# A two-layer relational graph convolution: 70 of 3126 tiles of source rows fetched by SyncE and ScalarE, a transfer per row

## The chip, the cores and the metric

The kernel runs on one core of a Trainium2 chip. The metric is the device time of one execution in microseconds; the time of a kernel is the median over several executions. A core has a matrix engine (TensorE, written PE, with its weight loads as PEld), a vector engine (VectorE, DVE), a scalar engine (ScalarE, ACT), a general one (GpSimd, POOL) and one for synchronisation (SyncE, SP). Each works through its own list of instructions in order. SP, ACT and POOL also issue the transfers (DMAs) between HBM and the on-chip memory SBUF; PE writes its results to PSUM.

## What is computed

There are N = 12500 nodes with C = 128 features, and E = 200000 edges sorted by their destination. Each edge has one of 10 types, the position of the largest of ten of its attributes. A layer takes, for each node and each type, the mean of the source nodes' features over the edges that arrive with that type, multiplies each mean by the type's 128x128 weights and sums over the types; to this come the node's own features times `root`, and a bias. Two such layers, with a relu between them, are followed by a sum with the input and a layer norm. Everything is in fp32.

```python
def _rgcn_layer(x, src, dst, edge_type, w_rel, root, bias):
    N = x.shape[0]
    seg = dst * NUM_REL + edge_type
    xs = x[src]
    sums = jax.ops.segment_sum(xs, seg, num_segments=N * NUM_REL)
    cnt = jax.ops.segment_sum(jnp.ones(seg.shape, x.dtype), seg, num_segments=N * NUM_REL)
    mean = (sums / jnp.maximum(cnt, 1.0)[:, None]).reshape(N, NUM_REL, -1)
    return jnp.einsum('nrd,rdo->no', mean, w_rel) + x @ root + bias
edge_type = jnp.argmax(msg[:, NODE_EMB_DIM:-NODE_EMB_DIM], axis=1).astype(jnp.int32)
h = jax.nn.relu(_rgcn_layer(x, src, dst, edge_type, w_rel1, root1, b1))
y = _rgcn_layer(h, src, dst, edge_type, w_rel2, root2, b2)
out = _layernorm(x + y)
```

## The kernel before

The edges are cut into 1563 tiles of 128, and the tiles into groups: 97 of 16 tiles, one of 8 and one of 3, so 99 a layer. A tile of the sorted edges reaches few nodes, and the kernel works in windows of 12 nodes by 10 types, 120 columns a tile. For a group it does this:

- `gather`: POOL issues one indirect transfer per tile (line 445), which brings the 128 source rows of 512 bytes from the table (`x` in the first layer, the stored hidden features `hD` in the second) into a tile of the buffer `g`. There are RING = 3 such buffers of 16 tiles.
- `sums`: DVE builds for each tile a matrix `oh` (line 461) that has the edge's weight, one over its count, in the column of its node and type; two `at` matrices (line 465) say where the windows lie. PE multiplies rows by `oh` into PSUM, `zp` (line 468), one matmul per tile. A fp32 matmul shows as two passes in the profile. The matmuls of a group are issued from j = 15 down to j = 0; 15 and the following ones are held in program order, and the waits for all gathers of the group are put on the first issued. ACT copies the sums out of PSUM in 4 pieces, `zs` (line 482).
- `project`, one group later: PE multiplies the sums by the weights of the 10 types, 20 matmuls into `pp` (line 494); ACT copies these out as `ms` (line 500).
- `add`, one group later again: two matmuls of `at` by `ms` (line 510) lay the windows out over 160 nodes, and DVE adds them to the running result `acc` (line 516) at an address that it loads into a register.

`layer` runs this over the groups. A gather into `g` must wait until the zp matmuls of three groups before have read that buffer; zp has one buffer in PSUM, `oh` and `zs` have two, `at` and `ms` three. When the edges of a block of 512 nodes are through, which is the case about every fourth group, the block is finished: SP loads its input rows (`rows_dma`, line 371), PE transposes them (line 386), ACT copies the transposed block out (`fT`, line 388), PE multiplies by `root` (line 400) and adds `acc` (line 401), ACT applies the relu (`hb`, line 414; first layer) or the square root of the norm (`rstd`, line 432; second), and SP stores the block. The first layer also has work on the edges' types and counts, spread over the groups in 13 chunks of 128 tiles: SP loads destinations, attributes and keys (lines 125, 290, 302, 330), ACT copies keys (line 335), DVE compares (line 341) and PE counts (lines 343 and 345).

The order on each engine is not the order of the text: a scheduler places the instructions, and only those marked with `keep_in_program_order` keep their places. A transfer issued by SP or ACT signals its end on one of 8 completion semaphores ("lanes") that the two engines use in turn, and an issue on a lane waits until the transfer before it on that lane has ended.

Of the kernel before, what the change touches and what calls it, by code (L numbers as in the profile page):

```python
# [9 lines left out]
F32 = mybir.dt.float32  # L10
BF16 = mybir.dt.bfloat16
I32 = mybir.dt.int32
# [4 lines left out]
DRAM = bass.MemoryType.DRAM  # L17
DVE = mybir.EngineType.DVE
SP = mybir.EngineType.SP

P = 128
NREL = 10
# [3 lines left out]
KW = NREL * WN  # L26
G = 16
QB = 4
HT = 8
HR = HT * WN  # L30
SW = 160
RING = 3
DB = 8
L = 40
CT = 128
# [8 lines left out]
def rgcn_resnorm_kernel(ctx: ExitStack, tc: tile.TileContext, x, src, dst, attr, w_rel1, root1, b1,  # L44
# [14 lines left out]
    nc = tc.nc  # L59
    N, C = x.shape  # L60
    E = src.shape[0]
    D = attr.shape[1]
    CE = CT * P
    NT = -(-E // P)
# [3 lines left out]
    t = NT // G * G  # L68
# [31 lines left out]
    fast = ctx.enter_context(ExitStack())  # L100
    keep = fast.enter_context(tc.tile_pool(name="keep", bufs=1))
    prep = fast.enter_context(tc.tile_pool(name="prep", bufs=1))
    eqp = fast.enter_context(tc.tile_pool(name="eqp", bufs=2))
    gpool = fast.enter_context(tc.tile_pool(name="gpool", bufs=RING))
    dpool = fast.enter_context(tc.tile_pool(name="dpool", bufs=2))
    zpool = fast.enter_context(tc.tile_pool(name="zpool", bufs=2))
    spool = fast.enter_context(tc.tile_pool(name="spool", bufs=3))
# [5 lines left out]
    idxE = keep.tile([P, NCH * CT], I32, name="idxE")  # L113
# [29 lines left out]
    def then(engine, ins):  # L143

        if engine in loaded:
            loaded.remove(engine)
            tc.keep_in_program_order(ins)
        return ins
# [81 lines left out]
    for k, (t, n) in list(enumerate(groups))[full:]:  # L230
        if k > full:
            nc.scalar.dma_start(bt[:, k:k + 1], bass.AP(dst.tensor, dst.offset + t * P, [[1, 1], [1, 1]]))
        m = n if t + n < NT else n - 1
# [91 lines left out]
    def count(c):  # L325
# [11 lines left out]
        R = P + L  # L337
        for d in range(1, L + 1, DB):
            eq = eqp.tile([P, DB, R], BF16, name="eqb")
            ahead = bass.AP(kh.tensor, kh.offset + d, [[kh.ap[0][0], p], [1, DB], [1, R]])  # L340
            nc.vector.tensor_tensor(eq[:p], kp[:p, None, :R].to_broadcast([p, DB, R]), ahead, op=ALU.is_equal)  # L341
            for k in range(0, DB, 4):
                nc.tensor.matmul(pc[:p], identb[:p, :p], eq[:p, k:k + 4, L:], start=(d + k == 1), stop=False)  # L343
# [18 lines left out]
    def rows_dma(sb, dr, k, store):  # L362
# [7 lines left out]
        for a, b in pairs:  # L370
            then("SP", nc.sync.dma_start(b, a) if store else nc.sync.dma_start(a, b))

# [67 lines left out]

    HELD = "clamped to a node on the chip"

    def gather(table, t0, n):
        g = gpool.tile([P, G, C], F32, name="g")
        return g, [then("POOL", nc.gpsimd.indirect_dma_start(  # L445
            out=g[:, j, :], out_offset=None, in_=table, in_offset=bass.IndirectOffsetOnAxis(
                ap=idxE[:, t0 + j:t0 + j + 1], axis=0))) for j in range(n)]

    whole = mybir.DependencyInfo(mybir.DependencyClass.Sync, mybir.DependencyReason.DATA)

    def halves(n):
        return [(h, min(HT, n - h * HT)) for h in range(-(-n // HT))]

    def sums(table, k, end):

        t0, n = groups[k]
        g, gathers = gather(table, t0, n)
        oh = dpool.tile([P, G, KW], F32, name="oh")
        for j in range(n):
            t = t0 + j  # L460
            then("DVE", nc.vector.tensor_scalar(oh[:, j, :], iotaP[:, :KW], keyE[:, t:t + 1], wE[:, t:t + 1],  # L461
                                                op0=ALU.is_equal, op1=ALU.mult))
        at = spool.tile([HR, 2, SW], F32, name="at")
        for h, _ in halves(n):
            nc.vector.tensor_scalar(at[:, h, :], iotaP[:HR], place[:, h, k:k + 1], None, op0=ALU.is_equal)  # L465
        zp = ps_z.tile([P, G // QB, YB], F32, name="zp")
        for j in range(n) if end else reversed(range(n)):
            m = nc.tensor.matmul(zp[:, j // QB, j % QB * KW:(j % QB + 1) * KW], g[:, j, :], oh[:, j, :],  # L468
                                 start=True, stop=True)
            then("PE", m)  # L470
            if end:
                continue
            if j < n - 1:
                tc.keep_in_program_order(m)
                continue

            for d in gathers[:j]:
                tc.add_manual_dep(m.ins, d.ins.name, whole, reason="one wait per group")
        zs = zpool.tile([P, NREL, G, WN], F32, name="zs")
        for b in range(-(-n // QB)):  # L480
            m = min(QB, n - b * QB)
            then("ACT", nc.scalar.activation(  # L482
                zs[:, :, b * QB:b * QB + m, :],
                zp[:, b, :m * KW].rearrange("c (j r n) -> c r j n", r=NREL, n=WN), AF.Copy))
        return k, zs, at

    def project(l, k, zs, at):

        n = groups[k][1]
        po = ps_o.tile([P, 2, C], F32, name="pp")  # L490
        ms = spool.tile([HR, 2, C], F32, name="ms")
        for h, m in halves(n):
            for r in range(NREL):
                nc.tensor.matmul(po[:m * WN, h], zs[:, r, h * HT:h * HT + m].rearrange("c j n -> c (j n)"),  # L494
                                 wsb[l][:, r, :], start=(r == 0), stop=(r == NREL - 1))
        if n % HT:
            for h, m in halves(n):
                nc.scalar.activation(ms[:m * WN, h], po[:m * WN, h], AF.Copy)
        else:
            nc.scalar.activation(ms[:, :n // HT], po[:HR, :n // HT], AF.Copy)  # L500
        return k, ms, at
# [3 lines left out]
    def add(k, ms, at):  # L505

        pa = ps_o.tile([P, 2, C], F32, name="pp").rearrange("p h c -> p (h c)")[:, :SW]
        parts = halves(groups[k][1])
        for h, m in parts:
            nc.tensor.matmul(pa, ms[:m * WN, h], at[:m * WN, h], start=(h == 0), stop=(h == len(parts) - 1))  # L510
        if not offs:
            offs.extend(nc.values_load_multi_w_load_instructions(
                bt[0:1, k:min(NG, k + 4)], engines=[DVE], min_val=0, max_val=N - 1,
                skip_runtime_bounds_check_because=HELD)[1])
        s = ds(offs.pop(0), SW)
        nc.vector.tensor_tensor(acc[:, s], acc[:, s], pa, op=ALU.add)  # L516

    def layer(table, l, finish, steps, flag_too=False):

        done = 0  # L520
        held, projected = [], []
        ready = flag = None

        def project_oldest():
            projected.append(project(l, *held.pop(0)))

        def add_oldest():
            nonlocal done
            k, ms, at = projected.pop(0)
            add(k, ms, at)  # L530
            while done < NBLK and sum(groups[k]) >= done_after(done):
                finish(done, ready if done == NBLK - 1 else block_in(done, l))
                done += 1

        for k in range(NG):
            end = k >= NG - 2
            if projected:
                add_oldest()
            if end:

                if held:
                    project_oldest()
                if not ready:
                    ready = block_in(NBLK - 1, l)
                    if flag_too:
                        loads, (flag,) = nc.values_load_multi_w_load_instructions(
                            flag_i[0:1, 0:1], min_val=0, max_val=1, skip_runtime_bounds_check_because=HELD)
                        for ld in loads:
                            tc.keep_in_program_order(ld)
                        loaded.update(("POOL", "DVE", "PE", "ACT", "SP"))  # L550
            held.append(sums(table, k, end))
            if end and projected:
                add_oldest()
            if len(held) > 1:
                project_oldest()
            if steps:
                till, left, s = steps[0]
                for _ in range(max(1, -(-left[0] // max(1, till - k)))):
                    left[0] -= 1
                    if next(s, steps) is steps:  # L560
                        steps.pop(0)
                        break
        while held or projected:
            if held:
                project_oldest()
            if projected:
                add_oldest()
        return flag
# [5 lines left out]
    def as_steps(f, c):  # L574
        f(c)
        yield
# [5 lines left out]
    for a in range(0, NPAD, YB):  # L582
        m = min(NPAD - a, YB)
# [7 lines left out]
    for c in range(1, NCH):  # L591
        s = [as_steps(sources, c + 1), types(c + 1)] if c + 1 < NCH else []
        todo.append((c * CT // G - 1, [8 + L // DB + 2], chain(*s, count(c))))
    layer(x, 0, hidden, todo)
    def flagged():

# [32 lines left out]
    def each_tile(before, stages):  # L629

        with tc.For_i(0, E, GT) as e:
# [30 lines left out]
            nw = nc.values_load(bw[0:1, 1:2], min_val=1, max_val=-(-N // W), skip_runtime_bounds_check_because=HELD)  # L662
            b0 = nc.values_load(bw[0:1, 0:1], engines=[DVE, SP], min_val=0, max_val=N - 1,
                                skip_runtime_bounds_check_because=HELD)
# [108 lines left out]
```

## Time and profile before

| what | value |
|---|---|
| median of 3 runs | 4760.23 us (4756.89 to 4762.15) |
| profiled execution | 4772.34 us, span 4770.4 us |
| mean granted TensorE clock | 0.739 |
| gathers | 3126, of 0.944 us each |
| traffic of POOL's queue (q0) | 100032 packets, 205.07 MB |
| HBM read, written | 262.28 MB, 13.60 MB |

The profile is taken by the hardware from one execution. A group line has the engine and the kernel's line, what is written and read, the count, the busy time and the mean of one instruction, and after a second bar the idle time ahead of those instructions with what ended most of it: "issue" where the engine waited for nothing that the profile shows, "remote" where the releasing event is on another engine but not identified, or the name of the instruction that released it. In the timeline a line is a run of like instructions: start, length, engine, line, and in brackets the idle time before it. An engine name with a q (SPq, ACTq) stands for the issue of transfers. The chain of waits, followed back from the end, puts 34% of the span down to releases that it can't name, 33% to PE, 21% to issue and 11% to DVE.

### The profile page before, as it was taken

The numbers are of one execution on the slowest core, as the hardware profiler recorded it, in microseconds if no ns is written. First come the engines' busy times: TensorE is split into PE (matmuls) and PEld (weight loads), VectorE is DVE, ScalarE is ACT, GpSimd is POOL, SyncE is SP. The second block draws the span as 40 slices with busy tenths as digits, with TensorE's granted clock in tenths as the row PEclk, the third lists the DMA queues.
The fourth block names the chain that finished last, engine by engine and source line by source line (L and its number), as shares of the span: only waits on it lengthen the run. The fifth ranks groups of instructions, "written<-read, shape, count | busy, mean of one in ns | idle before, by whom it ended". The sixth has DMA issues, their size and how long they took to land.

```text
span 4770.4 us, 43637 instructions
## 1 busy us (share of the span) xinstructions
PE 2759.5 (58%) x16162; PEld 2520.6 (53%) x16162; DVE 1511.5 (32%) x4652; ACT 527.0 (11%) x1136; POOL 2955.2 (62%) x3142
## 2 busy tenths in 40 slices
PE   2455556555655555666645555666655656565656
PEld 1455555555554545555544555555555555555556
DVE  5233333333333333333222222222222223222323
ACT  1011111111111101111110111111111111111111
POOL 5666665666656666666546666666666666666663
PEclk9677777777777777777776777777777777777778
DMA  4122122122221221212111211221222222222211
GB/s 141 44 79 74 50 74 74 50 75 62 61 77 47 75 62 51 57 48 52 46 49 46 54 52 51 53 56 51 52 56 53 52 52 58 51 52 52 58 52 40
DMA packets 180554, 279.00 MB, mean 58 GB/s; under 512 B 55623, under 2 KB 127190, under 8 KB 177206
## 3 DMA queue, kind: packets, MB, share of 16 engines
q0 software_dynamic: 100032, 205.07, 16.9%
q1 hardware_dynamic: 75428, 69.58, 4.6%
q8 instruction: 132, 2.16, 0.2%
q10 hardware_dynamic: 4872, 1.45, 0.1%
q14 instruction: 90, 0.74, 0.1%
HBM read 262.28 MB, written 13.60 MB: 58 GB/s over the span
## 4 chain that ended last, share of the span: by engine, by line
another core or an unknown queue 34%; PE 33%; issue 21%; DVE 11%; ACT 1%; DMA 0%; DVEq 0%; ACTq 0%; SPq 0%
PE pp L494 16%; PE zp L468 11%; DVE oh L461 7%; PE pp L510 2%; PE pf L401 1%; PE pf L400 1%; DVE at L465 1%; ACT zs L482 1%; DVE acc L516 1%; PE pf L343 0%; PE pf L345 0%; PE pf L386 0%; DVE o L436 0%; DVE st L429 0%
## 5 line engine op out<-in xcount | busy, mean ns | idle before, releaser
L445 POOL DMA_INDIRECT g<-in_x_dram,idxE x1563 | 1475.9, 944 | 911.2 <-issue 445.8
L445 POOL DMA_INDIRECT g<-hD,idxE x1563 | 1476.6, 945 | 865.3 <-issue 455.6
L494 PE MATMUL pp<-w,zs 128*96 128x128 f32 x7840 | 1358.2, 336 | 860.4 <-issue 722.1
L494 PEld LDWEIGHTS pp<-w,zs 128*96 128x96 f32 x7840 | 1232.0, 212 | 982.9 <-issue 834.6
L461 DVE TENSOR_SCALAR oh<-bank,keyE,wE 128x120 f32<-128x120 f32 x3126 | 1000.1, 400 | 644.6 <-remote 576.6
L468 PE MATMUL zp<-oh,g 128*128 128x120 f32 x6252 | 1033.5, 325 | 293.5 <-issue 259.9
L468 PEld LDWEIGHTS zp<-oh,g 128*128 128x128 f32 x6252 | 983.1, 240 | 314.0 <-issue 292.5
L482 ACT ACTIVATE zs<-zp 128x480 f32<-128x480 f32 (+1 forms) x782 | 382.9, 575 | 2167.7 <-remote 1912.9
L516 DVE TENSOR_TENSOR acc<-acc,pp 128x160 f32 x198 | 63.7, 322 | 1634.4 <-remote 1043.0
L510 PE MATMUL pp<-at,ms 96*128 96x160 f32 (+1 forms) x784 | 198.1, 386 | 591.1 <-issue 405.0
L510 PEld LDWEIGHTS pp<-at,ms 96*128 96x128 f32 (+1 forms) x784 | 142.5, 232 | 633.8 <-issue 437.1
L500 ACT ACTIVATE ms<-pp 96x256 f32<-96x256 f32 x196 | 74.1, 378 | 1241.3 <-remote 861.3
L341 DVE TENSOR_TENSOR eqb<-pf,kh 128x1344 bf16<-128x1344 f32 (+1 forms) x65 | 100.6, 1552 | 181.4 <-PE pf L345 82.3
L400 PE MATMUL pf<-root,fT 128*128 128x128 f32 x388 | 110.1, 379 | 79.0 <-issue 49.1
L401 PE MATMUL pf<-ident,a 128*128 128x128 f32 x392 | 114.0, 388 | 60.3 <-DVE a L395 22.0
L400 PEld LDWEIGHTS pf<-root,fT 128*128 128x128 f32 x388 | 87.0, 276 | 91.2 <-issue 55.8
L465 DVE TENSOR_SCALAR at<-bank,place 96x160 f32<-96x160 f32 x392 | 131.9, 376 | 0.0
L401 PEld LDWEIGHTS pf<-ident,a 128*128 128x128 f32 x392 | 90.7, 285 | 68.6 <-issue 24.6
L426 DVE TENSOR_TENSOR v<-pf,xb 128x512 f32<-128x512 f32 (+1 forms) x28 | 17.4, 620 | 243.2 <-remote 238.3
L348 DVE TENSOR_REDUCE wp<-pf 128x128 f32<-128x512 f32 (+1 forms) x13 | 9.0, 691 | 182.9 <-remote 175.5
L343 PE MATMUL pf<-eqb,identb 128*128 128x512 bf16 (+1 forms) x130 | 50.5, 388 | 17.9 <-DVE f L320 17.0
L388 ACT ACTIVATE fT<-pf 128x512 f32<-128x512 f32 (+1 forms) x56 | 30.2, 539 | 207.1 <-remote 151.3
(107 smaller groups left out, 483.0 us busy)
## 6 DMA issues: line engine op xcount, KB each, us to landing
m<-in_edge_attr_dram SPq DMA_DIRECT2D x24, 1344.0 KB
g<-in_x_dram,idxE POOLq DMA_INDIRECT x1563
g<-hD,idxE POOLq DMA_INDIRECT x1563
xb<-in_x_dram SPq DMA_DIRECT2D x46, 256.0 KB
hD<-hb SPq DMA_DIRECT2D x23, 256.0 KB
hb<-hD SPq DMA_DIRECT2D x23, 256.0 KB
out_dram<-o SPq DMA_DIRECT2D x23, 256.0 KB
w<-in_L_gnn_w_rel_dram ACTq DMA_DIRECT2D x2, 640.0 KB
```

The source lines that it names most:

```text
L341: nc.vector.tensor_tensor(eq[:p], kp[:p, None, :R].to_broadcast([p, DB, R]), ahead, op=ALU.is_equal)
L400: nc.tensor.matmul(pr[:h, t, :], fT[:, t * P:t * P + h], rsb[l], start=True, stop=False)
L401: nc.tensor.matmul(pr[:h, t, :], a[:, t * P:t * P + h], ident, start=False, stop=True)
L445: return g, [then("POOL", nc.gpsimd.indirect_dma_start(out=g[:, j, :], out_offset=None, in_=table, in_offset=bass.IndirectOffsetOnAxis(ap= ...
L461: then("DVE", nc.vector.tensor_scalar(oh[:, j, :], iotaP[:, :KW], keyE[:, t:t + 1], wE[:, t:t + 1], op0=ALU.is_equal, op1=ALU.mult))
L465: nc.vector.tensor_scalar(at[:, h, :], iotaP[:HR], place[:, h, k:k + 1], None, op0=ALU.is_equal)
L468: m = nc.tensor.matmul(zp[:, j // QB, j % QB * KW:(j % QB + 1) * KW], g[:, j, :], oh[:, j, :], start=True, stop=True)
L482: then("ACT", nc.scalar.activation(zs[:, :, b * QB:b * QB + m, :], zp[:, b, :m * KW].rearrange("c (j r n) -> c r j n", r=NREL, n=WN), AF.C ...
L494: nc.tensor.matmul(po[:m * WN, h], zs[:, r, h * HT:h * HT + m].rearrange("c j n -> c (j n)"), wsb[l][:, r, :], start=(r == 0), stop=(r == ...
L500: nc.scalar.activation(ms[:, :n // HT], po[:HR, :n // HT], AF.Copy)
L510: nc.tensor.matmul(pa, ms[:m * WN, h], at[:m * WN, h], start=(h == 0), stop=(h == len(parts) - 1))
L516: nc.vector.tensor_tensor(acc[:, s], acc[:, s], pa, op=ALU.add)
```

## The change

Some tiles are no longer gathered by POOL. In each layer SP takes tile 64, 128, ... 1536 (24 tiles, always the tile j = 0 of every fourth group) and ACT takes tile 160, 288, ... 1440 (11 tiles, j = 0 of every eighth group, in groups that have no SP tile). For such a tile the engine loads its 128 source numbers into one SBUF row, reads them eight at a time into registers, and issues 128 transfers of one row of 512 bytes each, at the table's row that the register names, into a `rows` tile of which there are two per engine. The issue is spread over the groups ahead of the one that needs the tile: 32 rows per group on SP and 16 per group on ACT, in the order of the program's text. In all 70 of 3126 gathers go, and 6144 row transfers on SP and 2816 on ACT come, with 70 loads of sources and 1120 loads of registers. The zp matmul of j = 0 in these groups reads `rows` in place of `g`.

```diff
+ACT = mybir.EngineType.Activation
...
 RING = 3
+MS = 64
+MA = 128
+RB = 8
...
+    rpool = fast.enter_context(tc.tile_pool(name="rpool", bufs=2))
...
+    by_rows = {}
+
+    def fetch(table, engine, eng, tag, tiles, M):
+
+        lists = {}
+
+        def sources_of(t):
+            lo = min(t * P, E - P)
+            lists[t] = rpool.tile([1, P], I32, name="sr" + tag)
+            then(tag, eng.dma_start(lists[t], src[lo:lo + P].rearrange("(o e) -> o e", o=1)))
+
+        step = 0
+        sources_of(tiles[0])
+        for t in tiles:
+            while step < (t - M) // G:
+                step += 1
+                yield
+            sr = lists.pop(t)
+            if t + M in tiles:
+                sources_of(t + M)
+            r = by_rows[t] = rpool.tile([P, C], F32, name="rows" + tag)
+            for e in range(0, P, RB):
+                loads, at = nc.values_load_multi_w_load_instructions(
+                    sr[0:1, e:e + RB], engines=[engine], min_val=0, max_val=N - 1,
+                    skip_runtime_bounds_check_because="sources are nodes")
+                for ld in loads:
+                    tc.keep_in_program_order(ld)
+                for i in range(RB):
+                    eng.dma_start(r[e + i:e + i + 1, :], table[ds(at[i], 1), :])
+                if (e + RB) % (P * G // M) == 0:
+                    step += 1
+                    yield
+
     def gather(table, t0, n):
         g = gpool.tile([P, G, C], F32, name="g")
-        return g, [then("POOL", nc.gpsimd.indirect_dma_start(
+        return g, {j: then("POOL", nc.gpsimd.indirect_dma_start(
             out=g[:, j, :], out_offset=None, in_=table, in_offset=bass.IndirectOffsetOnAxis(
-                ap=idxE[:, t0 + j:t0 + j + 1], axis=0))) for j in range(n)]
+                ap=idxE[:, t0 + j:t0 + j + 1], axis=0))) for j in range(n) if t0 + j not in by_rows}
 
     whole = mybir.DependencyInfo(mybir.DependencyClass.Sync, mybir.DependencyReason.DATA)
 
...
             nc.vector.tensor_scalar(at[:, h, :], iotaP[:HR], place[:, h, k:k + 1], None, op0=ALU.is_equal)
         zp = ps_z.tile([P, G // QB, YB], F32, name="zp")
         for j in range(n) if end else reversed(range(n)):
-            m = nc.tensor.matmul(zp[:, j // QB, j % QB * KW:(j % QB + 1) * KW], g[:, j, :], oh[:, j, :],
+            rows = by_rows.pop(t0 + j) if t0 + j in by_rows else g[:, j, :]
+            m = nc.tensor.matmul(zp[:, j // QB, j % QB * KW:(j % QB + 1) * KW], rows, oh[:, j, :],
                                  start=True, stop=True)
             then("PE", m)
             if end:
...
                 tc.keep_in_program_order(m)
                 continue
 
-            for d in gathers[:j]:
+            for d in [d for i, d in gathers.items() if i < j]:
                 tc.add_manual_dep(m.ins, d.ins.name, whole, reason="one wait per group")
         zs = zpool.tile([P, NREL, G, WN], F32, name="zs")
         for b in range(-(-n // QB)):
...
                 finish(done, ready if done == NBLK - 1 else block_in(done, l))
                 done += 1
 
+        fetches = [fetch(table, SP, nc.sync, "SP", range(MS, NT - G, MS), MS),
+                   fetch(table, ACT, nc.scalar, "ACT", range(MA + MS // 2, NT - G, MA), MA)]
         for k in range(NG):
+            for f in fetches:
+                next(f, None)
             end = k >= NG - 2
             if projected:
                 add_oldest()
```

## The prediction

> **What bounds the kernel now.** I read the busy table first (median of the runs shown 4760.23 us; the profiled execution is 4772.34 us with a span of 4770.4, and every sum below is made against this span).
>
> ```profile
> PE 2759.5 (58%) x16162; PEld 2520.6 (53%) x16162; DVE 1511.5 (32%) x4652; ACT 527.0 (11%) x1136; POOL 2955.2 (62%) x3142
> L445 POOL DMA_INDIRECT g<-in_x_dram,idxE x1563 | 1475.9, 944 | 911.2 <-issue 445.8
> L445 POOL DMA_INDIRECT g<-hD,idxE x1563 | 1476.6, 945 | 865.3 <-issue 455.6
> L482 ACT ACTIVATE zs<-zp 128x480 f32<-128x480 f32 (+1 forms) x782 | 382.9, 575 | 2167.7 <-remote 1912.9
> ```
>
> No engine is full; POOL is the busiest. Its gathers are 0.944 us each, with about 0.3 us of issue before the next, so 1.249 us apart; half of its idle time is that issue, the other half pauses. ACT's copies of the sums out of PSUM (zs) idle for "remote", mostly. Second, the timeline of two groups of 16 gathers (start, length, engine, line; in brackets the idle time before):
>
> ```profile
> 2508.67 0.94 POOL L445 DMA_INDIRECT g<-hD,idxE  x1 [0.30 <-issue]
> 2512.82 1.96 ACT L482 ACTIVATE zs<-zp 128x480 f32<-128x480 f32 x4 [21.14 <-remote]
> 2512.82 2.58 DVE L461 TENSOR_SCALAR oh<-bank,keyE,wE 128x120 f32<-128x120 f32 x8 [17.47 <-remote]
> 2513.05 0.94 POOL L445 DMA_INDIRECT g<-hD,idxE  x1 [3.44 <-remote]
> ...
> 2519.17 4.92 PE L468 MATMUL zp<-oh,g 128*128 128x120 f32 x32
> ...
> 2523.93 1.69 PE L494 MATMUL pp<-w,zs 128*96 128x128 f32 x14
> ...
> 2530.08 0.80 PE L494 MATMUL pp<-w,zs 128*96 128x128 f32 x3 [2.25 <-issue]
> ...
> 2535.87 1.96 ACT L482 ACTIVATE zs<-zp 128x480 f32<-128x480 f32 x4 [20.84 <-remote]
> 2536.05 0.94 POOL L445 DMA_INDIRECT g<-hD,idxE  x1 [3.31 <-remote]
> ```
>
> The reader is to see one **release** per group: zs on ACT, oh on DVE and the next gather on POOL start together, at 2512.82 and again 23.05 us later. Between them POOL makes 16 x 1.249 = 20.0 us of gathers and then waits 3.3 us. The zp matmuls that ought to release them were over at 2519.17 + 4.92 = 2524.1, yet the release came 11.8 us later, 3.3 us after POOL had gone quiet. PE has two paces: for some 12 us behind a release its passes follow at 0.12 to 0.2 us (14 in 1.69), and from then until POOL stops they come singly with gaps near 0.7, 1.4 and 2.1 us: 10 passes in the 9.9 us from 2525.85 to 2535.74. So the cycle is POOL's 20.0 us plus 3.3. Third, the waits of POOL over the second layer:
>
> ```profile
> POOL g L445 <- issue: 455.6, 1464, 5.1
> POOL g L445 <- remote: 229.0, 64, 8.1
> POOL g L445 <- PE zp L468: 147.8, 30, 8.3
> ```
>
> Pauses cost 229.0 + 147.8 = 377 us of a layer (some 94 of them, 4.0 us each): groups in which a block of nodes is also finished (every fourth) pause 5 to 6 us and last about 25; the two zs copies at 2792.45 and 2817.84 stand 25.4 apart around one. In the first layer the counting chunks bring pauses of 8 to 10.7.
>
> **The change, part by part.**
>
> *Removed:* 35 gathers a layer, 70 in all. One is worth 1.249 us where POOL sets the cycle: at most 87 us. Where the pause rather than POOL ends last, it may be worth nothing; of the 48 tiles that go to SP 36 lie in groups with a long pause, of the 22 that go to ACT one does. (I laid each tile's group against POOL's pause behind the same group in the trace.) Lower end, the other 33 alone: 41.
>
> *Added:* per tile one list of sources (one DMA), 16 register loads of 8 addresses each, and 128 one-row transfers, each with a register instruction before it. No such transfer is in the trace. One-partition DMAs are issued in 0.22 us (SP L221) to 0.47, pairs of larger ones on SP follow at 0.38 to 0.48 while POOL gathers; a register instruction on DVE takes 0.07, a load of a few registers there 0.34, or 0.04 per row. So a row is 0.33 to 0.55 us; I take **0.45**, and 0.70, PE's slow step, as the far bound. Each row also waits for one of 8 completion lanes that both queues share: a load of 128 rows of 512 bytes lands 2.0 us after its issue here, so 8 lanes pass a row per 0.25 us, or 0.5 for each queue while both send, which is hardly dearer than taken. The rows for these two:
>
> ```profile
> 1.66 0.22 SPq L221 DMA_DIRECT2D KD<-negs  x1
> 0.83 0.40 SPq L125 DMA_DIRECT2D s_i<-in_src_dram  x1
> ```
>
> ```profile
> 2.82 0.28 DVE L162 CAST s_f<-s_i 128x128 f32<-128x128 int32 x1 [1.18 <-DMA s_i<-in_src_dram]
> ```
>
> A tile is 58 us of SP's time. SP has a tile every 4 groups, 93 us, so it fits with 35 us to spare; at 0.70 it is 90, with nothing to spare. ACT's tile is 58 us in 8 groups, 16 rows to a group and 7.2 us, where ACT is busy 11%. What covers rows is the wait of their tile, two buffers deep, some 4 to 8 groups. The DMAs of SP that now stand behind row bursts (m, d, kh, xb, hb, the stores) are due a block later; the worst, kh behind 57 rows, is 26 us late against a chunk of 8 groups, 185 us. I cost that at nothing; if it is not covered it is one pause of that length per chunk, 12 x 26 = 312 at most.
>
> *Moved.* This is what decides. In the order in which the built program's instructions stand on each engine, the zp matmul that reads the fetched rows (j = 0, the last of the group, now waiting for the row lanes) no longer follows the other 15. In each of the 48 groups with an SP tile it stands behind the 20 pp matmuls and the 2 additions of the group before, and behind that the block's transposes and root. The release of that group therefore now waits for pp, for ms on ACT, for the addition, and for whatever ACT does before these. ACT's order in the second layer repeats over 8 groups: in one of two SP groups ("heavy", 12 a layer) ms stands behind 16 rows, and fT, which root needs, behind 32 more; in the other ("light") ms stands behind 16 rows and zs behind 16.
>
> - Heavy group, second layer: before pp is done PE makes 30 zp passes, 4 additions, 40 pp: 74, of which 60 in 12.8 us (the quick stretch above) and 14 at 1.0 per us (this window) to 1.75: 21 to 27, taken 22. Then ms 0.4, 32 rows 14.4, the list, a register load and fT 2.0, transposes, root and zp 1.5: release after 40.3 us. The next release follows shortly, as its zp waits for little, so POOL then goes 20.0 without a pause. Pair: 60.3 against 25.4 + 23.05 = 48.4, so **+11.9**. Low: rows at 0.33 (-3.8) and a second pause skipped (-3.5): +4.6. High: rows at 0.70 (+8.0), pp at 27: +24.9.
> - Light group: 16 rows (7.2) ahead of ms lie beside pp; zs 7.2 later, but its pause is regained after it: +0.5, from -3 to +6.
> - First layer, where counting runs: 12 groups with 16 rows and a second fT (0.6) ahead of the release, +8, from +2 to +16; 12 with 16 rows ahead of zs, beside PE's slow part: +3, from 0 to +7.2.
> - ACT-tile groups: zp is not moved far; 22 x 1.249 = -27, from -27 to 0.
>
> Sum: 12 x 11.9 + 12 x 0.5 + 12 x 8 + 12 x 3 - 27 = 143 + 6 + 96 + 36 - 27 = **+254**. The lane waits add 315 semaphore instructions on PE; PE's take 0.05 us in the trace: 16 us spread over stretches in which it waits anyway, nothing.
>
> A rule of the Trainium skill speaks against the change: "DMA: Bandwidth & Descriptors", section "Bandwidth", holds transfers under 64 KB to be dominated by their descriptors, and a row is 512 bytes. The trace has a load of 64 KB, which lands in 2.0 us, and none as small as a row, so no run here shows it yet; by the rule alone the sum would stand, since the rows' landing is covered two tiles ahead. The same page, section "Latency and other measured facts", gives a register load a floor of about 0.6 us against the 0.34 of the trace; with it a row would be 0.03 us dearer and the heavy groups 12 x 32 x 0.03 = 12 us longer.
>
> **The rivals.**
>
> 1. *The gather is saved and the rest hidden.* For it: ACT idles 89%, SP nearly always, and POOL's pitch is in every period. Against it: the place of j = 0 behind pp. It decides if a heavy group's release comes within the 25.4 us of before, which takes PE at its quick pace throughout (74 x 0.16 = 12 us) and rows of 0.3 us: 12 + 0.4 + 9.6 + 3.5 = 25.5. Then 41 to 87 us are saved: 4683 to 4729 on the span, 4673 to 4719 by the median, middle 4695.
> 2. *No change.* The pause grows by what the gather gives, since the release is tied to more than POOL. It needs the heavy groups at +4.6 and the light ones and the first layer at nothing: 12 x 4.6 - 41 = +14, within 0.3%.
> 3. *SP or ACT falls behind.* If a row comes to more than 93/128 = 0.73 us on SP, the rows set the period: at 1.0 us a tile is 128 us in place of 93, 48 x 35 = 1680 us longer, about 6440; at the high ends of the terms above, 299 + 72 + 192 + 86 = 5420. PE's step of 0.7 us speaks for it, SP's pairs at 0.4 us in the same stretches against it.
> 4. *The rows are not used*, or arrive but the gathers remain: the built program shows 3056 gathers and the matmuls on rows, so hardly.
>
> **How the numbers follow.** The terms between their ends (low: 55 - 36 + 24 + 0 - 27 = +16, so 4786; high as above): 0.54. Beyond (3): 0.19. Nothing (2 and 4): 0.05. Rival 1: 0.22. The likeliest is 4770.4 + 254 = 5024 on the span, and by the median, 10 lower, about 5015. The likeliest's own range is 4786 to 5420. The range given, 4690 to 5420, leaves out 3 and the lower half of 1; with 3 cut at the sum of the high ends I hold some 2 in 10 outside. A difference under 0.2% of 4760, 9.5 us, can't be told from none: faster 0.22, same 0.04, slower 0.74.
>
> **What would show it.** POOL's gathers at 3056 with the same 0.944 us; in every second SP group a wait of POOL of over 15 us that ends with zp, preceded by row issues on ACT between ms and fT; the group after it without a pause. Wrong if POOL's pauses stay near 3.4 us in SP groups (rival 1), if the row pitch is over 0.7 us (3), or if the first layer grows without the second. I would also be wrong if the 3.3 us between POOL's end and the release comes from the gathers' own landing.

## The result, and the profile after

The changed kernel takes 7264.71 us (median of 4 runs, 7253.16 to 7270.53) against 4758.56 us before (4754.01 to 4762.15): ratio 1.527, 95% interval 1.5251 to 1.5289. It is slower, as forecast, but the forecast was 5015 us with a range to 5420. The excess is 2506 us where 254 were worked out.

The kernel before turned out to have two speeds, and this matters for every number below. The experiments were run in six groups, each on one chip. In the first three (two chips) the kernel before took 4750 to 4763 us, as in the profile that the prediction read; in the last three (two other chips) it took 3974 to 3978 us. Runs are compared only with the kernel before on the same chip. I call the first **stepped** chips, for the 0.7 us steps that the prediction saw in PE's passes, and the others **even** ones. As no chip was met in both kinds and all stepped groups came before all even ones, the names stand for the groups: that it is the chip which makes the difference, and not something that changed meanwhile, isn't shown. The result above is from a stepped one.

The busy table of the changed kernel, and the groups that answer to those shown of before:

```profile
span 7251.4 us, 72080 instructions
...
PE 2652.5 (37%) x16162; PEld 2442.5 (34%) x16162; DVE 1532.5 (21%) x4652; ACT 528.5 (7%) x1136; POOL 2893.7 (40%) x3072
...
L483 POOL DMA_INDIRECT g<-in_x_dram,idxE x1528 | 1445.5, 946 | 2153.9 <-PE zp L507 1492.4
L483 POOL DMA_INDIRECT g<-hD,idxE x1528 | 1445.3, 946 | 2136.7 <-PE zp L507 1609.5
...
L521 ACT ACTIVATE zs<-zp 128x480 f32<-128x480 f32 (+1 forms) x782 | 383.2, 575 | 2919.4 <-PE zp L507 1650.3
```

POOL made its 3056 gathers at nearly the same 0.946 us each (0.944 before); no engine has much more compute (DVE, with 21 us, the most). POOL's idle time went from 1776 to 4291 us, and most of it now ends with zp. The instructions rose by 28,443, from 43,637 to 72,080 (first line of each page). Both layers grew by the same: from first to last gather the first layer took 2385 us before and 3598 after, the second 2309 and 3523.

One stretch of the second layer, as the timeline has it for POOL, then for SP, then for PE (start, length, engine, line, and in brackets the idle time before):

```profile
5026.04 0.95 POOL L483 DMA_INDIRECT g<-hD,idxE  x1 [0.31 <-issue]
5073.02 0.95 POOL L483 DMA_INDIRECT g<-hD,idxE  x1 [46.03 <-PE zp L507]
```

```profile
5009.67 20.80 SPq L476 DMA_DIRECT2D rowsSP<-hD  x15
```

```profile
5006.85 4.53 PE L533 MATMUL pp<-w,zs 128*96 128x128 f32 x40
5029.90 1.43 PE L549 MATMUL pp<-at,ms 96*128 96x160 f32 x4 [18.51 <-ACT ms L539]
5063.71 0.76 PE L507 MATMUL zp<-oh,rowsSP 128*128 128x120 f32 x2 [32.38 <-DMA rowsSP<-hD]
...
5067.03 5.72 PE L507 MATMUL zp<-oh,g 128*128 128x120 f32 x32
```

While POOL gathers (the last gather of its burst starts at 5026.04) and for 3.5 us more SP gets 15 rows out in 20.8 us, 1.39 us each. POOL then stands 46 us: the gather at 5073.02 waits for the 32 passes of zp that start at 5067.03, these come behind the matmul on SP's rows at 5063.71, and that one had waited 32 us for rows. Over the whole run SP's rows stand 0.91 us apart on average (gaps over 8 us left out): 0.58 while POOL has been idle for 3.5 us or more, 2.5 us from the twelfth microsecond of a burst on. In the trace each row is three instructions (an addition on registers, a move, the transfer), and late in a burst steps of 0.70 us, or of a multiple, fall within or between all three. The prediction had allowed 0.70 us per row.

SP's waits for another queue's transfers, in us, times and the longest:

```profile
SPq L476 <- DMA rowsACT<-hD: 571.4, 138, 22.1
SPq L476 <- DMA rowsACT<-in_x_dram: 313.9, 105, 28.4
```

So 885 us of SP's time goes on completion lanes whose turn belongs to a row of ACT that has not been issued or has not landed.

### The profile page after: what moved, and what is told of

It is laid out like the page before. It is cut to its first block, busy times and chain, and to the rows that moved or that the text cites. A ratio compares the mean times of both kernels' runs of the same rounds, so it can differ in the third digit from the quotient of the medians.

```text
span 7251.4 us, 72080 instructions
## 1 busy us (share of the span) xinstructions
PE 2652.5 (37%) x16162; PEld 2442.5 (34%) x16162; DVE 1532.5 (21%) x4652; ACT 528.5 (7%) x1136; POOL 2893.7 (40%) x3072
## 5 line engine op out<-in xcount | busy, mean ns | idle before, releaser
L483 POOL DMA_INDIRECT g<-in_x_dram,idxE x1528 | 1445.5, 946 | 2153.9 <-PE zp L507 1492.4
L483 POOL DMA_INDIRECT g<-hD,idxE x1528 | 1445.3, 946 | 2136.7 <-PE zp L507 1609.5
L533 PE MATMUL pp<-w,zs 128*96 128x128 f32 x7840 | 1126.2, 303 | 500.1 <-issue 355.3
L533 PEld LDWEIGHTS pp<-w,zs 128*96 128x96 f32 x7840 | 1040.8, 186 | 577.8 <-issue 400.7
L507 PEld LDWEIGHTS zp<-oh,g 128*128 128x128 f32 x6112 | 1022.1, 260 | 542.1 <-DVE oh L499 451.7
L549 PE MATMUL pp<-at,ms 96*128 96x160 f32 (+1 forms) x784 | 258.1, 478 | 2087.5 <-ACT ms L539 1355.7
L549 PEld LDWEIGHTS pp<-at,ms 96*128 96x128 f32 (+1 forms) x784 | 185.2, 298 | 2126.5 <-ACT ms L539 1377.9
L507 PE MATMUL zp<-oh,rowsSP 128*128 128x120 f32 x96 | 32.5, 437 | 779.4 <-DMA rowsSP<-hD 378.5
L507 PEld LDWEIGHTS zp<-oh,rowsSP 128*128 128x128 f32 x96 | 22.2, 287 | 791.5 <-issue 484.6
L391 PE MATMUL pf<-ident,hb 128*128 128x128 f32 x97 | 26.7, 422 | 236.9 <-DMA hb<-hD 236.9
```

Source lines behind the costliest of these rows:

```text
L483: return g, {j: then("POOL", nc.gpsimd.indirect_dma_start(out=g[:, j, :], out_offset=None, in_=table, in_offset=bass.IndirectOffsetOnAxis( ...
```

## The experiments

Three theories stood at the start: A, SP's pace (rows held up by the gathers); B, the shared lanes; C, the moved j = 0 matmul of the prediction. Later came D, the place of rows behind other transfers in SP's queue, and E, a cost of every instruction. Times are device times, and those of the table further down the spans of the profiled executions; single runs unless an interval is given.

### One part at a time: SP alone, constant addresses, unread rows, the order held

Only SP fetches:

```diff
-        fetches = [fetch(table, SP, nc.sync, "SP", range(MS, NT - G, MS), MS),
-                   fetch(table, ACT, nc.scalar, "ACT", range(MA + MS // 2, NT - G, MA), MA)]
+        fetches = [fetch(table, SP, nc.sync, "SP", range(MS, NT - G, MS), MS)]
```

> Three theories. A: SP is the bound; a row is three instructions (register arithmetic, register move, transfer), and while POOL gathers each of them is held up, so that a row takes 2 to 2.8 us in place of 0.41. B: SP stands still for lanes that wait for ACT's rows (885 us of its waits in the changed kernel). C: the place of the j = 0 matmul behind pp and ACT's rows, as predicted. Here ACT fetches nothing. A: only the lane waits go, 18 of 152 us per four groups, so 6300 to 6700 us. B: under 5500 us. C: no rows on ACT ahead of ms and fT, so some 4900 us.

Constant addresses in place of registers, on both queues, and no loads of registers:

```diff
-                    eng.dma_start(r[e + i:e + i + 1, :], table[ds(at[i], 1), :])
+                    n0 = (t * 7 + (e + i) * 97) % N
+                    eng.dma_start(r[e + i:e + i + 1, :], table[n0:n0 + 1, :])
```

> The rows come from constant addresses (other rows than the reference wants), one instruction per row in place of three and no register loads; number of transfers, lanes and tiles as in the changed kernel. A: SP's 128 rows need 80 to 95 us per four groups, so 4750 to 5200 us. B: the 885 us of lane waits stay, 5600 us or more. C: rows of 0.26 us on ACT, nothing else changed: 6800 to 7100 us.

Rows that nobody reads:

```diff
-            r = by_rows[t] = rpool.tile([P, C], F32, name="rows" + tag)
+            r = rpool.tile([P, C], F32, name="rows" + tag)
```

> All 3126 gathers are kept and the rows are fetched beside them, but no matmul reads them, so zp waits for no row and keeps its place. A: SP still has to issue 6144 rows, with its loads and stores of the blocks among them, and POOL gathers more of the time: 6500 us or more. B: 5600 us or more. C: 4760 to 4800 us.

The pp matmuls held in the program's order:

```diff
-                nc.tensor.matmul(po[:m * WN, h], zs[:, r, h * HT:h * HT + m].rearrange("c j n -> c (j n)"),
-                                 wsb[l][:, r, :], start=(r == 0), stop=(r == NREL - 1))
+                tc.keep_in_program_order(nc.tensor.matmul(
+                    po[:m * WN, h], zs[:, r, h * HT:h * HT + m].rearrange("c j n -> c (j n)"),
+                    wsb[l][:, r, :], start=(r == 0), stop=(r == NREL - 1)))
```

> The pp matmuls are held in program order, so that the j = 0 matmul on rows stands with the other 15 of its group and not behind the 20 pp matmuls of the group before. A: SP's rows set the period as before: 6700 to 7300 us. B: the same as A. C: 4700 to 5000 us.

These four shared a chip on which the kernel before took 4757 us. Measured: SP alone 6510 us, constant addresses 5898, unread rows 7233, order held 6935. The unread rows decide most. No matmul waits for a row there, zp keeps its old place, all 3126 gathers are made, and the kernel is as slow as the changed one:

```profile
span 7231.2 us, 71852 instructions
...
PE 2611.8 (36%) x16162; PEld 2430.9 (34%) x16162; DVE 1529.9 (21%) x4652; ACT 526.1 (7%) x1136; POOL 2953.0 (41%) x3142
```

So the wait of zp for its rows, and with it C, is not the main cause; the run with the order held puts C's part at 7265 - 6935 = 330 us. SP alone fell where A put it, and takes 755 us off, close to the 885 us of lane waits of B. Constant addresses missed A's number by 700 us: rows came at 0.54 us on average, enough for SP to keep its pace, and the time stayed at 5898, above the 5600 that B had set.

### SP alone with constant addresses, ACT alone, the gain alone, and rows without gathers

> Rows from constant addresses as in the second run, and on SP alone (ACT fetches nothing). A with lanes as the second cost: SP's rows at some 0.6 us are 77 us per tile, under the 93 us of four groups, and no lane waits for ACT: 4680 to 4900 us. If it stays above 5500 us, neither the instructions of a row nor the lanes account for what the run with constant addresses kept (5898 us).

> SP fetches nothing; ACT's 22 tiles stay as they are. A: ACT has 16 rows to a group, 7 us where it idles and up to 40 us where POOL gathers, in the queue ahead of ms, zs and fT: 4800 to 5300 us. B alone (waiting between the two queues): 4700 to 4760 us, since nobody waits for a lane of the other. C: only SP groups had the matmul moved: 4730 to 4760 us.

For the third the tiles read one that was loaded once:

```diff
+        for t in (*range(MS, NT - G, MS), *range(MA + MS // 2, NT - G, MA)):
+            by_rows[t] = still
```

> The 70 gathers are left out and nothing fetches in their place: those matmuls read a tile that was loaded once (so 8960 edges of each run's 400000 take other rows). The gain that the change was after, alone: 4670 to 4720 us by the price of 1.249 us a gather; 4740 to 4765 us if the pauses take it back.

For the fourth nothing is gathered either (`gather` returns such a tile, 16 wide, and no transfers), and only SP fetches:

> SP fetches its 48 tiles with registers as in the changed kernel, and no matmul reads them; no tile is gathered, all matmuls read one tile that was loaded once. Shows whether POOL's gathers are what stretches a row. A: every row at 0.41 us and a load of registers of some 1 us per 8, 0.53 us a row, 3300 to 3700 us in all; PE's passes run close. If the rows still come at about 0.9 us, the gathers are not the cause: above 5500 us.

On this chip the kernel before took 4750 us. Measured: 5562, 5356, 4700 and 3803 us. With the waits for ACT's lanes, registers and ACT's rows all gone SP alone still costs 812 us, above the 5500 that I had set as the mark for an unknown cause. The longest of SP's waits, 1330 us of its 5560, was then for a block's result to store:

```profile
SPq L376 <- DVE o L441: 1329.9, 28, 138.0
```

ACT alone, with 22 tiles, costs 606 us, more than any of the three theories had set. Leaving the gathers out and fetching nothing gains 49 us in one run, inside the 41 to 87 that were priced; that is about all the change could have won on a stepped chip. Without any gathers the time is somewhat above the 3300 to 3700 us expected and far below the 5500, and SP's rows came close together, 93 in 48.5 us, 0.52 each:

```profile
2911.52 48.50 SPq L476 DMA_DIRECT2D rowsSP<-hD  x93
```

So it is POOL's gathers that stretch a row, as A has it. Starts of PE's passes that lie over 0.6 us apart fell from 7% (kernel before) to 1%.

### Half the tiles, and rows ahead of time

`MS = 128` and no tiles on ACT:

> SP fetches every 128th tile (12 a layer), ACT none, rows from registers. A: 128 rows at the 0.93 us measured with gathers are 119 us of the 186 us of eight groups, so SP is no longer the bound, and what remains is the place of the last rows behind a block's store in SP's queue (theory D, 18 us per SP tile in the run with constant addresses on SP alone): 24 x 18 - 24 x 1.249, 4740 to 5160 us. If the time goes with the number of rows whatever SP's pace: half of the way from the kernel before to the run with SP alone, 5630 us.

Constant addresses on SP alone, each tile four groups earlier:

```diff
-            while step < (t - M) // G:
+            while step < (t - 2 * M) // G:
```

> As the run with constant addresses on SP alone, but each tile's rows are issued four groups earlier, with three buffers, so that a store that waits in SP's queue no longer holds back rows that are due (the first tile of a layer stays with POOL). D: 4680 to 4780 us. If 5400 us or more, the loss of that run lies elsewhere (C, or traffic).

Half the tiles, eight groups earlier; and the same with the pp matmuls in the program's order:

> Every 128th tile on SP with rows from registers (11 a layer), issued eight groups earlier, three buffers. A with D: 4715 to 4780 us. With C alone, the moved matmul costs some part of the 330 us that holding the order gave: 4800 to 4900 us.

> As the run before, and the pp matmuls held in program order. All theories: 4715 to 4760 us, if 22 gathers give 22 x 1.249 = 27 us, and no more than this to be had.

Before: 4763 us. Measured: 5630, 5546, 5520 (ratio 1.1578, 1.1557 to 1.1599) and 5451 us (1.1436, 1.1411 to 1.1461). A and D fall as main causes here. With half the tiles a tile's rows come to 137 us (1.07 each) of the 227 us that eight groups last, and SP stands waiting, among others for a block to use what it has loaded:

```profile
SPq L376 <- DVE v L431: 587.7, 8, 88.9
SPq L376 <- PE pf L391: 442.4, 17, 96.4
```

Yet the cost halves with the rows, to the very 5630 us of the other alternative; rows that are ready four groups ahead change 5562 into 5546. So the cost goes with what is added, the rows and their instructions, whoever waits for them. All stepped runs with gathers, against the page of before (4770.4 us, 43,637 instructions):

| run | instructions added | us added | us per instruction |
|---|---|---|---|
| changed kernel | 28,443 | 2481 | 0.087 |
| unread rows | 28,215 | 2461 | 0.087 |
| order held | 28,412 | 2163 | 0.076 |
| SP alone | 19,641 | 1738 | 0.088 |
| half the tiles | 9,796 | 858 | 0.088 |
| half, earlier | 8,940 | 762 | 0.085 |
| half, earlier, order held | 8,932 | 686 | 0.077 |
| ACT alone | 8,965 | 584 | 0.065 |
| constant addresses | 9,334 | 1126 | 0.121 |
| constant, SP alone | 6,532 | 789 | 0.121 |
| constant, earlier | 6,209 | 774 | 0.125 |

A fit over these, the kernel before and the run with the gathers left out gives 0.129 us per transfer that SP or ACT issues and 0.065 us per other instruction, and meets each span within 3.3%. That is theory E. Measured by the cost alone it is rougher: the 3.3% are 225 of 2163 us with the order held and some 140 of 584 with ACT alone. A fit by rows, 0.27 us for one with an address from a register and 0.13 for one without, meets the spans as well, so the runs on stepped chips don't tell a price per instruction from a price per row.

### Instructions without rows, fewer instructions, no gathers

Only loads of sources into registers, two at a time:

> All 3126 gathers as in the kernel before; SP brings in the 48 lists of sources and loads them into registers, two at a time, 3072 register loads in all, and no row is transferred. Theory E (each instruction, on whatever engine, costs some 0.065 us while POOL gathers): 4757 + 3072 x 0.065 + 48 x 0.129 = 4960 us, 4880 to 5050. If transfers of rows are what costs, or SP's pace (64 loads are 58 us of 93): 4750 to 4780 us.

The kernel before with `oh` built in 4 instructions per group in place of 16:

```diff
-        for j in range(n):
-            t = t0 + j
-            then("DVE", nc.vector.tensor_scalar(oh[:, j, :], iotaP[:, :KW], keyE[:, t:t + 1], wE[:, t:t + 1],
-                                                op0=ALU.is_equal, op1=ALU.mult))
+        for a in range(0, n, HT):
+            b = min(n, a + HT)
+            wide3 = [P, b - a, KW]
+            then("DVE", nc.vector.tensor_tensor(oh[:, a:b, :], iotaP[:, None, :KW].to_broadcast(wide3),
+                 keyE[:, t0 + a:t0 + b, None].to_broadcast(wide3), op=ALU.is_equal))
+            nc.vector.tensor_tensor(oh[:, a:b, :], oh[:, a:b, :],
+                 wE[:, t0 + a:t0 + b, None].to_broadcast(wide3), op=ALU.mult)
```

> The kernel before, with the 16 DVE instructions that build oh for a group replaced by 4 (two halves, a comparison and a product each): 2330 instructions fewer, about the same DVE time, no rows. E: 4757 - 2330 x 0.065 = 4605 us, 4560 to 4680. If POOL's 20 us and a fixed pause set the period, 4740 to 4770 us; more, if the longer first piece of oh delays zp.

> The kernel before without any gather: every matmul reads one tile that was loaded once. The base of the next run. E's rate (9 to 10 instructions per us) needs POOL's gathers: 40500 instructions then go at PE's own pace, 2400 to 3200 us. If the rate holds without gathers: 4000 us or more.

> As the run before, and SP fetches every 128th tile (24 in all) row by row with registers; no matmul reads them. SP needs 3072 x 0.54 = 1660 us, less than the base. If the cost per instruction needs the gathers: within 150 us of the run before. If not: 3072 x 0.28 = 860 us more, as with gathers.

These four fell on an even chip: the kernel before took 3978 us, 780 less than on the others. Measured: loads 3996 us, `oh` merged 4075 (ratio 1.0247, 1.023 to 1.0265), no gathers 1960 (below the 2400 to 3200 expected), no gathers with rows 2328. There the 3072 register loads cost 18 us in one run, 0.006 each: E does not hold on this chip, and the runs that were to test it say nothing of the stepped ones. What they show is the other kind of chip. The run with the loads, which has all gathers, has POOL's waits like this:

```profile
POOL g L479 <- issue: 917.5, 3011, 0.3
POOL g L479 <- DMA hD<-hb: 31.4, 1, 31.4
...
POOL g L479 <- PE zp L503: 12.4, 2, 12.1
```

The 3.3 us behind every sixteenth gather, 377 us of a layer in the prediction, are gone; 3126 gathers at 1.25 us are 3908 of its 3994 us, and starts of PE's passes over 0.6 us apart are 1.7%. No gathers with rows is 368 us above no gathers, 0.12 us a row, between the 150 and the 860 expected. PE is busy 73 us longer there, at a granted clock of 0.93 in place of 0.994, and idles 293 us more; DVE waits 110 us for `xb`, which SP loads behind the rows, and not at all for it without rows. So SP's order has a part in it, and that a row has a price of its own on an even chip is not shown.

### The changed kernel on an even chip

> The changed kernel once more, against the kernel before on the same chip. Where the kernel before takes some 4760 us (other engines held up in steps while POOL gathers): 7265 us, 1.527, by theory E. Where it takes some 3980 us (no steps): a row costs 0.54 us in all, a tile of SP 69 us of the 80 us of four groups, POOL would save at most 87 us; what is left against that is the moved matmul behind pp and ACT's rows (C): 3890 to 4200 us. If it takes over 5500 us there too, the cost of the rows has nothing to do with the steps.

It fell on an even chip. Before 3974 us, after 4305: ratio 1.084 (1.0822 to 1.0858), 105 us above the 3890 to 4200 expected. The same program that costs 2506 us more on a stepped chip costs 332 us here. That this lies inside the prediction's own range for its terms (16 to 649) is luck: as the rest of this part shows, about half of it goes with a load that the prediction had put at nothing. Rows stand 0.58 us apart on SP, 0.59 on ACT. POOL's bursts now run over many groups, and its pauses are few: idle stretches of 18 to 30 us between two gathers in the counting chunks of the first layer, one of 4 to 10 us per eight groups in the second, as the idle time of POOL in the two layers shows:

```profile
L483 POOL DMA_INDIRECT g<-in_x_dram,idxE x1528 | 1442.8, 944 | 789.4 <-issue 474.5
L483 POOL DMA_INDIRECT g<-hD,idxE x1528 | 1442.9, 944 | 568.2 <-issue 442.9
```

The second layer's gathers take 1957 us from first to last, against 1954 in the run with loads on an even chip. The loss is in the first layer (2230 against 1967 us). A pause of the first layer on POOL, on SP's queue and on DVE:

```profile
1005.06 0.94 POOL L483 DMA_INDIRECT g<-in_x_dram,idxE  x1 [28.14 <-PE zp L507]
```

```profile
968.39 16.00 SPq L476 DMA_DIRECT2D rowsSP<-in_x_dram  x32
984.48 0.37 SPq L295 DMA_DIRECT2D m<-in_edge_attr_dram  x1
```

```profile
990.31 0.83 DVE L271 TENSOR_REDUCE bank<-m 128x64 f32<-128x640 f32 x1 [35.53 <-DMA m<-in_edge_attr_dram]
...
994.40 4.74 DVE L499 TENSOR_SCALAR oh<-bank,keyE,wE 128x120 f32<-128x120 f32 x15
```

Read from below: the `oh` instructions of a group (the last line has 15 of the 16) stand on DVE behind the type work on `m`; DVE waited 35.5 us for `m`; and `m` was issued only when SP had the rows ahead of it in its queue out. PE needs `oh`, POOL needs PE: 28 us.

The two profiles of this one program also show where the steps lie. Here are the addition on registers and the transfer of a row on SP, with the shortest, median and longest length in ns, on the stepped chip and then on the even one:

```profile
L476 SPq FUSED_REGOPS  x6144: 2/37/1407, 17.1 to 7220.8; - x199
L476 SPq DMA_DIRECT2D rowsSP<-hD x3072: 2/228/1409, 3659.8 to 7220.9; - x192
```

```profile
L476 SPq FUSED_REGOPS  x6144: 37/37/51, 17.0 to 4268.9; - x199
L476 SPq DMA_DIRECT2D rowsSP<-hD x3072: 224/227/305, 2287.4 to 4269.0; - x192
```

On the even chip no issue of a row is recorded with less than 224 ns; on the stepped one some have 2, and others 1409. So at a step the recorded start of an instruction can be late as well as its end.

Last, the changed kernel with `m` taken out of SP's queue and given a buffer for each half:

```diff
-            m = prep.tile([P, H * D], F32, name="m")
-            nc.sync.dma_start(m[:n], bass.AP(attr.tensor, attr.offset + (c * CE + o) * D, [[P * D, n], [1, H * D]]))
+            m = prep.tile([P, H * D], F32, name=f"m{o}")
+            nc.gpsimd.dma_start(m[:n], bass.AP(attr.tensor, attr.offset + (c * CE + o) * D, [[P * D, n], [1, H * D]]))
```

> The changed kernel with the loads of the edges' attributes (m, 26 transfers) issued by POOL between its gathers, into a buffer for each half, and no longer by SP behind the rows. Where the kernel before takes some 3980 us: if m behind the rows makes the 28 us pauses, 12 of them go and 24 x 1.2 us of issue come on POOL: 3960 to 4060 us; if they come from the rows that zp waits for, 4250 to 4320. Where the kernel before takes some 4760 us: theory E, cost per instruction, leaves 6850 to 7270 us; if the queue order of SP makes the loss there too, under 5500.

Again an even chip: before 3977 us, this 4135, ratio 1.0402 (1.0383 to 1.042). Half of the 332 us go, between the two ranges expected. The run doesn't tell the queue's part from that of the second buffer. The long pauses became ones of at most 11 us, but for one of 24; one of them, again ended by zp:

```profile
674.40 0.94 POOL L483 DMA_INDIRECT g<-in_x_dram,idxE  x1 [9.70 <-PE zp L507]
```

What the other half is made of I did not separate.

## Why the prediction was wrong

- **Direction: right.** Slower, at 0.74.
- **The price of a row, the step that failed.** The prediction took 0.45 us, with 0.70 as the far bound, and charged it to the engine that issues the row, there to be hidden or not. Undisturbed that is near: 0.41 us on SP and 0.39 on ACT (medians), 0.52 to 0.59 with the register loads, of which one for eight rows took 0.80 us where 0.34 was taken. On a stepped chip PE's step falls on each of a row's three instructions while POOL gathers, so rows come at 0.91 us on average and 2.5 late in a burst. The step was in the page read, in PE's passes, and was allowed once per row. Nor does the charge stay with the issuing engine: the changed kernel is 2481 us longer for its 8960 rows, 0.28 us each, and with half of SP's tiles it is 0.28 us a row too, though SP then waits. The SP pairs at 0.4 us that spoke against the step are single instructions, with no address from a register.
- **What hides the rows.** The prediction let "the wait of their tile, two buffers deep" cover them. It was not needed: rows that nobody reads cost as much. The cost did not come by the tile's wait, and rows issued four or eight groups earlier (5546 and 5520 us) hardly cost less.
- **Rival 3** (SP falls behind from 0.73 us a row, 0.19) named the right side and its point was passed: in the changed kernel the mean distance of SP's rows is 0.91 us, and from the first to the last they reach over 7205 of 7251 us. But its mechanism was not the main one, since with half of the rows SP had time to spare and the cost was halved (858 of 1738 us).
- **The moved matmul**, which "decides" by the text, with +143 of the +254 us in the second layer's heavy groups. On a stepped chip holding the order gave 330 us of 2506, where the terms of the moved matmul come to 143 + 6 + 96 + 36 = 281. That it is the same cost isn't shown: by the gathers' first and last, the first layer lost 104 us and the second 223. On an even chip the second layer cost nothing, its pauses of about 5 us per eight groups being about what the gathers saved. The place in the order was read rightly, and it isn't what makes the change cost 2506 us.
- **Loads behind rows in SP's queue: "I cost that at nothing", with 12 x 26 = 312 us at most.** On the even chip it was there. The load was `m`, not `kh`: 18 to 30 us a pause, and taking it out of the queue, with a second buffer, gave 4305 - 4135 = 170 us.
- **Shared lanes**, taken as "hardly dearer": 885 us of SP's waits in the changed kernel, and 755 us less without ACT's rows. As those rows take their instructions with them, the two costs are not separated (8802 instructions at 0.088 would be 775 us).
- **The gain:** 49 us measured, 41 to 87 priced. Right.
- **Pauses behind the gathers.** The prediction left open where POOL's 3.3 us came from and named "the gathers' own landing" as what would make it wrong. On even chips the gathers land too, and there is no such pause; it goes with the steps.
- **Two readings.** The prediction says that no load in its trace is as small as a row. There are some of 0.5 KB and less, among them the biases; what the trace lacks is a row at an address from a register. And PE's slow passes do not all come singly: the line at 2530.08 has three in 0.80 us. No term of the sum rests on either.

What the steps are stays open. Shown is that they need POOL's gathers (rows at 0.54 us without them), that one group of runs has them and another not with the same program, and that on stepped chips the time grows with the rows and their instructions, on SP or ACT, read or unread. Not shown is that an instruction without a transfer costs the same on a stepped chip, since both runs meant for it fell on an even one. The Trainium skill offers one candidate: "NOTIFIC — the notification-queue block", section "Overflow: three behaviours, one of which stalls the engine", says that the block which writes the records of executed instructions holds its producers back when its own pipeline is full rather than lose a record, and that this can throttle an engine. A limit on such records, shared by all engines, would give a cost per instruction, and recorded lengths of 2 ns beside 224 would fit a start that is noted late, but no run here measures that block. Every execution listed in these runs has a recorded span and clock, so there is none without recording to compare with: whether the steps, and with them most of the 2506 us, are there when nothing is recorded stays open too.

## What to carry to other kernels

Look for steps first: where a profile has engines moving in equal steps, price an added transfer with every instruction that it brings, on the account of the whole kernel and not only of the issuing queue, for there it wasn't free however idle the engine that took it. Run the kernel before again beside each change, since the same program may go with the steps or without. Before work goes to an idle queue, list what stands behind it there: a load that feeds another engine's in-order list is late by all that was put ahead of it. And no version that fetches the rows beats the kernel before here; on a stepped chip the gathers alone were worth 49 us, so 8960 transfers had to cost under 0.006 us each to pay.

## What the runs showed of the hardware

- The same kernel takes 4750 to 4763 us in some groups of runs and 3974 to 3978 in others, on other chips, each within 0.3%. A ratio holds for its group: the change is 1.527 on the one kind and 1.084 on the other.
- On an even chip a transfer of one row at an address from a register is issued in 0.23 us and stands 0.41 us from the next on SP, 0.39 on ACT; a load of eight registers takes 0.80 us. At a constant address a row stands 0.295 us from the next (median, on a stepped chip).
- Merging 16 DVE instructions into 4 made the kernel 2.5% slower on an even chip, where POOL sets the time: the gathers took 0.978 us each, against 0.946 in the run with the loads.

```profile
L445 POOL DMA_INDIRECT g<-hD,idxE x1563 | 1528.7, 978 | 496.1 <-issue 470.8
```
